# Second attention: the order of a block's direct and turned products, of VectorE's sums, and of the rows' transposes

## The chip, the cores and the metric

The kernel runs on one core of a Trainium2 chip. The metric is the device time of one execution in microseconds. A core has several engines with a queue each: TensorE (PE; its weight loads are listed as PEld), VectorE (DVE), ScalarE (ACT), GpSimd (POOL) and SyncE (SP), the last of which only starts DMAs here.

## The reference, cut to what matters

The network has a convolutional attention layer, then a plain self-attention over tokens, then a spectral filter layer. The change concerns the middle one. For each of two batches it takes normalised tokens `x` of shape 4096 x 128 and computes:

```python
scores = jnp.einsum('bsd,btd->bst', x, x)
attn_weights = jax.nn.softmax(scores, axis=-1)
return jnp.einsum('bst,btd->bsd', attn_weights, x)
```

Since queries, keys and values are the same tokens, the matrix of scores is symmetric. After the exponential, which here takes a fixed shift instead of a maximum, it still is: a 512 x 512 block (j, i) above the diagonal, turned, is the block (i, j) below it. The division by the row sums comes last.

## The kernel before, in words

The second attention is the function `attend16`. A batch has 4096 tokens in eight tiles of 512, so it has 36 blocks (j, i) with i from j to 7; 28 lie above the diagonal and 8 on it. They are numbered in the order of the list `order`: row j = 0 with i = 0 to 7, then row 1 with i = 1 to 7, and so on. The times below count the blocks of both batches through, 0 to 71.

For one block:

- `scores` works in two halves h and makes in all: twelve products `y` (three for each of four groups of 128 rows, since each operand is a sum of two half-precision parts), four exponentials `ey` on ScalarE that also give row sums into `den`, two casts to the first half-precision part of `pair` on ScalarE, and two subtractions on VectorE that give the second part (line 1199).
- `turn` (only above the diagonal) starts two transposing DMAs on SP's queue, one for each part of `pair`, into the tile `eT` (line 1204). `eT` has two buffers, `pair` two, `ey` two.
- `direct` makes twelve products `od` with `pair`, in one PSUM bank with the tag `acc1`, and adds them to `oT` for tile i on VectorE (line 1225, or a copy at 1227 in row 0).
- `across` (only above the diagonal) uses the turned block: VectorE makes four sums `both` over `eT` (line 1232), whose purpose is the row sums for `den`, and TensorE twelve products `oa` over `eT`, which add up over a row in the PSUM bank with the tag `acc0`.
- `close` ends a row j: it adds `oa` to `oT` (line 1246), sums `den` and takes reciprocals, transposes the four groups of the row on TensorE (`o`, line 1252) and adds them, scaled, to the tokens with four operations `tok` on VectorE (line 1255). It then calls `closed(j)`, which sets off or opens work for the neighbouring stages.

The loop over n runs two passes longer than there are blocks. In a pass it traces the scores and the turning of block n, then `across` of block n - 2 (and `close` where this ends a row), then `direct` of block n - 1. After each of these steps it takes one step from a generator `beside`: in batch 0 the normalising of the other batch and leftovers of the first layer, in batch 1 the feed of the third layer.

The order in which the code traces is not by itself the order in which an engine runs. The kernel is written in a framework that orders each engine's queue by rank (the order of tracing) and by the time at which it takes inputs to be there; only instructions wrapped in `keep_in_program_order` are held to the code's order on their engine. Within `attend16` none is. [...]

Of the kernel before, what the change touches and what calls it, by code (L numbers as in the profile page):

```python
# [19 lines left out]
ALU = mybir.AluOpType  # L20
# [8 lines left out]
NQ = L // 512  # L29
# [47 lines left out]
def conv_attn_hybrid(ctx: ExitStack, tc: tile.TileContext, io):  # L77
    nc = tc.nc
# [38 lines left out]
    def chain(*parts):  # L117
        for p in parts:
            yield from p
# [638 lines left out]
    def layers(st, layer0, in_halves):  # L758
# [415 lines left out]
        def attend16(b, p, beside, closed):  # L1174

            den = p.tile([P, NT, NQ], F32, tag="den", name=f"den{b}")
            oT = p.tile([P, NQ, 512], F32, tag="oT", name=f"oT{b}")

            def scores(j, i, pair, h):
                ps = psum.tile([P, 2, 512], F32, tag="st", name=f"y{b}_{j}_{i}_{h}")  # L1180
                e = p.tile([P, 2, 512], F32, tag="e", name=f"ey{b}_{j}_{i}_{h}", bufs=2)
                for q in range(2):
                    t = 4 * j + 2 * h + q
                    for n, (a, c) in enumerate(((hiT, hiT), (hiT, loT), (loT, hiT))):
                        nc.tensor.matmul(  # L1185
                            ps[:, q, :],
                            a[0][:, bass.ts(t, P)],
                            c[0][:, bass.ts(i, 512)],
                            start=(n == 0),
                            stop=(n == 2),  # L1190
                        )
                for q in range(2):
                    t = 4 * j + 2 * h + q
                    nc.scalar.activation(  # L1194
                        e[:, q, :], ps[:, q, :], AF.Exp, bias=nshift16, accum_out=den[:, t, i : i + 1]
                    )
                own = slice(2 * h, 2 * h + 2)
                nc.scalar.copy(pair[:, 0, own], e)  # L1198
                nc.vector.tensor_tensor(pair[:, 1, own], e, pair[:, 0, own], ALU.subtract)  # L1199

            def turn(j, i, pair):
                eT = p.tile([P, 2, 4, 4, P], F16, tag="eT", name=f"eT{b}_{j}_{i}", bufs=2)
                for n in range(2):
                    nc.sync.dma_start_transpose(
                        eT[:, n].rearrange("p t u k -> p (t u) k"), pair[:, n].rearrange("p t q -> p (t q)")
                    )
                return eT

            def weigh(acc, first, pair, start, stop):
                for t in range(4):  # L1210
                    own = bass.ts(first + t, P)
                    for n, (a, m) in enumerate(((hi, 0), (lo, 0), (hi, 1))):
                        nc.tensor.matmul(  # L1213
                            acc,
                            a[0][:, own],
                            pair(m, t),
                            start=(start and t == 0 and n == 0),
                            stop=(stop and t == 3 and n == 2),
                        )

            def direct(j, i, pair):
                acc = psum.tile([P, 512], F32, tag="acc1", name=f"od{b}_{j}_{i}", bufs=1)
                weigh(acc, 4 * j, lambda m, t: pair[:, m, t, :], True, True)
                if j:
                    nc.vector.tensor_tensor(oT[:, i, :], acc, oT[:, i, :], ALU.add)  # L1225
                else:
                    nc.vector.tensor_copy(oT[:, i, :], acc)

            def across(j, i, eT, acc):
                for u in range(4):  # L1230
                    both = p.tile([P, 4, P], F16, tag="both", name=f"both{b}_{j}_{i}_{u}", bufs=1)
                    nc.vector.scalar_tensor_tensor(  # L1232
                        both,
                        eT[:, 0, :, u, :],
                        1.0,
                        eT[:, 1, :, u, :],
                        ALU.mult,
                        ALU.add,
                        accum_out=den[:, 4 * i + u, j : j + 1],
                    )  # L1240
                weigh(acc, 4 * i, lambda m, u: eT[:, m, :, u, :], i == j + 1, i == NQ - 1)

            def close(j, acc):
                fin = oT[:, j, :]
                if acc is not None:
                    nc.vector.tensor_tensor(fin, acc, fin, ALU.add)
                rden = p.tile([P, 4], F32, tag="rden", name=f"rden{b}_{j}")
                nc.vector.reduce_sum(rden, den[:, 4 * j : 4 * j + 4, :], axis=AX.X)
                nc.vector.reciprocal(rden, rden)
                pt = bank(f"o{b}_{j}")  # L1250
                for t in range(4):
                    nc.tensor.transpose(pt[:, bass.ts(t, P)], fin[:, bass.ts(t, P)], ident)
                for t in range(4):
                    dst = tok[b][:, 4 * j + t, :]
                    nc.vector.scalar_tensor_tensor(
                        dst, pt[:, bass.ts(t, P)], rden[:, t : t + 1], dst, ALU.mult, ALU.add
                    )
                closed(j)

            order = [(j, i) for j in range(NQ) for i in range(j, NQ)]  # L1260
            pairs, turned, accs = {}, {}, {}
            for n in range(len(order) + 2):
                if n < len(order):
                    j, i = order[n]
                    pair = p.tile([P, 2, 4, 512], F16, tag="pair", name=f"pair{b}_{j}_{i}", bufs=2)
                    for h in range(2):
                        scores(j, i, pair, h)
                        next(beside, None)
                    pairs[n] = pair
                    if i > j:  # L1270
                        turned[n] = turn(j, i, pair)
                if n > 1:
                    j, i = order[n - 2]
                    if i > j:
                        if i == j + 1:
                            accs[j] = psum.tile([P, 512], F32, tag="acc0", name=f"oa{b}_{j}", bufs=1)
                        across(j, i, turned.pop(n - 2), accs[j])
                        if i == NQ - 1:
                            close(j, accs[j])
                    elif i == NQ - 1:  # L1280
                        close(j, None)
                    next(beside, None)
                if 0 < n <= len(order):
                    direct(*order[n - 1], pairs.pop(n - 1))
                    next(beside, None)
            for _ in beside:
                pass

# [93 lines left out]
        with ExitStack() as l1:  # L1382
# [3 lines left out]
            with ExitStack() as part:  # L1386
# [18 lines left out]
                def closed(j):  # L1405
                    gate[0] = j + 1
# [8 lines left out]
                own = (rest16(p),) if in_halves else (filters(p, fw), matrices(p))  # L1415
                steps = chain(left, stats.steps(), *own, normalise(1, stats, stage, gate))
                (attend16(0, p1, steps, closed) if in_halves else attend(0, p1, steps, closed, ready))
            right0.close()
            if in_halves:
# [274 lines left out]
        beside = chain([None] * WC, feed(1, late_pool, one_bank, fw, fed))  # L1694
        steps = 0
        for b in range(B):
            for ro in range(2):
# [3 lines left out]
                for ch in range(NCH):  # L1701
                    acc = pc.tile([P, 512], F32, tag="acc", name=f"m{b}_{ro}_{ch}")
                    for s in range(2):
                        u = f"{b}_{ro}_{ch}_{s}"
# [19 lines left out]
                beside = back(b, ro, oh, outs, late_pool)  # L1724
                if in_halves and (b, ro) == (0, 1):
                    beside = chain(beside, guard(one_bank))
# [136 lines left out]
```

## Time and profile before

| what | value |
|---|---|
| median of 3 runs | 2777.88 us (2777.81 to 2810.39) |
| the profiled execution | 2786.72 us, of which its span 2784.9 us |
| mean granted TensorE clock in it | 0.977 |
| second attention in it | about 1046 to 1724 us |
| after it | the third layer's products, which wait for a load of `tables_b` |

The page gives each engine's busy time; the answers of the trace used below give, for a stretch of the execution, the busy times by window, the waits (which instruction waited for which, in us, how often, longest), the instructions in order of time, and the chain of work that ended last. In names like `oT<-od,oT` the written tile stands to the left of the arrow. L1232 is line 1232.

### The profile page before, as it was taken

How to read it: one execution, taken by the hardware profiler on the slowest of the kernel's cores; microseconds unless marked ns; L12 is line 12 of the kernel's file. 1: busy time of each engine (PE TensorE's matmuls, PEld its weight loads, DVE VectorE, ACT ScalarE, POOL GpSimd, SP SyncE). 2: the span in 40 equal slices, each digit the busy share in tenths (PEclk: the TensorE clock that was granted, in tenths of full speed). 3: DMA queues.
4: the chain of work that ended last, by engine and by line, in shares of the span. 5: the costliest groups of instructions: out<-in, count | busy, mean ns of one | idle time of the engine just before them, and what ended most of it. 6: DMA issues, size and time to landing. Idle time of an engine off the chain costs nothing.

```text
span 2784.9 us, 32561 instructions
## 1 busy us (share of the span) xinstructions
PE 2588.1 (93%) x11955; PEld 1276.1 (46%) x11955; DVE 1668.5 (60%) x2946; ACT 1841.3 (66%) x2059; POOL 432.5 (16%) x711
## 2 busy tenths in 40 slices
PE   5999999999998996999989988898789999999998
PEld 3555555555544452444434443343344445445444
DVE  5256564246267225767886567575456666666664
ACT  4999999999998894556644555454345555555553
POOL 2022121012124201100043100111111111111110
PEclk9999999999999997999999998999999999999999
DMA  4122220012014307655375654666666666655662
GB/s 144 35 65 67 65 65 20 7 50 74 22 39 94 67 5 135 115 107 105 69 144 110 126 96 91 154 174 156 149 167 165 200 192 181 179 206 179 185 188 87
DMA packets 351051, 311.92 MB, mean 112 GB/s; under 512 B 292816, under 2 KB 303200, under 8 KB 334432
## 3 DMA queue, kind: packets, MB, share of 16 engines
q1 hardware_dynamic: 295376, 231.71, 32.6%
q0 software_dynamic: 52512, 74.81, 11.2%
q10 hardware_dynamic: 2992, 3.22, 0.4%
q8 instruction: 96, 1.57, 0.2%
q14 instruction: 75, 0.61, 0.1%
HBM read 212.53 MB, written 23.33 MB: 85 GB/s over the span
## 4 chain that ended last, share of the span: by engine, by line
PE 30%; DMA 13%; DVE 7%; issue 1%; ACT 1%; POOL 0%; SPq 0%; DVEq 0%; ACTq 0%; POOLq 0%
PE m L1557 19%; PE cv L1541 6%; DMA eT<-pair 5%; DMA tables_b<-tables 3%; DVE pair L1199 3%; DMA base<-oc 2%; DVE both L1232 2%; PE ar L1312 1%; DMA had<-base 1%; DVE x L1549 1%; PE bk L1669 1%; DMA tables_a<-tables 1%; DMA rows<-uh 1%; PE od L1213 1%; PE pf L1328 0%
## 5 line engine op out<-in xcount | busy, mean ns | idle before, releaser
L465 ACT ACTIVATE e<-s 128x1536 f16<-128x1536 f32 (+1 forms) x704 | 938.4, 1427 | 52.9 <-PE s L209 48.3
L1549 DVE TENSOR_TENSOR x<-cv,x 128x1024 f16<-128x1024 f32 x512 | 602.3, 1219 | 302.9 <-ACT x L1548 302.9
L1548 ACT CAST x<-cv 128x1024 f16<-128x1024 f32 x512 | 493.7, 1017 | 404.4 <-PE cv L1541 389.5
L1557 PE MATMUL m<-x,mxr 128*128 128x512 f16 x2048 | 622.5, 381 | 0.0
L209 PE MATMUL acc<-e,v 128*97 128x512 f16 x2048 | 559.0, 380 | 16.4 <-DVE accs L413 13.7
L209 PE MATMUL s<-qs,ks 128*128 128x512 f16 x2048 | 559.7, 380 | 7.9 <-ACT e L465 4.3
L1557 PE MATMUL m<-x,mxl 128*128 128x512 f16 x1024 | 391.4, 382 | 3.3 <-DVE oh L1564 3.2
L209 PEld LDWEIGHTS <-v 128*97 128x97 bf16 x2048 | 255.4, 125 | 229.8 <-issue 28.9
L1194 ACT ACTIVATE ey<-y,nshift 128x512 f32<-128x512 f32 x288 | 196.0, 685 | 225.3 <-PE y L1185 135.9
L1557 PEld LDWEIGHTS <-mxr 128*128 128x128 f16 x2048 | 201.3, 98 | 242.8 <-issue 5.3
L209 PEld LDWEIGHTS <-ks 128*128 128x128 f16 x2048 | 201.0, 99 | 229.6 <-issue 46.8
L1478 POOL DMA_DIRECT2D tokens<-rows x252 | 152.9, 611 | 845.5 <-PE cv L1541 819.8
L1232 DVE SCALAR_TENSOR_TENSOR both<-eT 128x512 f16<-128x512 f16 x224 | 153.6, 686 | 135.2 <-DMA eT<-pair 124.5
L1213 PE MATMUL od<-pair,hi 128*128 128x512 f16 x576 | 189.6, 391 | 30.0 <-DVE oT L1225 15.1
L1185 PE MATMUL y<-bothT 128*128 128x512 f16 x864 | 206.5, 381 | 4.0 <-ACT ey L1194 3.0
L1199 DVE TENSOR_TENSOR pair<-ey,pair 128x1024 f16<-128x1024 f32 x144 | 175.4, 1218 | 16.0 <-ACT pair L1198 15.6
L413 DVE COPY accs<-acc 97x512 f32<-97x512 f32 x64 | 44.1, 689 | 227.3 <-PE acc L209 227.1
L1541 PEld LDWEIGHTS <-tokens 128*128 128x128 f16 x1024 | 100.6, 99 | 164.5 <-issue 68.1
L1213 PEld LDWEIGHTS <-hi 128*128 128x128 f16 x1024 | 102.6, 100 | 146.2 <-issue 35.1
L1198 ACT CAST pair<-ey 128x1024 f16<-128x1024 f32 x144 | 150.2, 1043 | 24.6 <-DMA eT<-pair 11.4
L1557 PEld LDWEIGHTS <-mxl 128*128 128x128 f16 x1024 | 101.0, 99 | 131.6 <-DVE oh L1564 10.0
L1213 PE MATMUL oa<-eT,hi 128*128 128x512 f16 x448 | 146.6, 389 | 14.3 <-DMA eT<-pair 14.3
(221 smaller groups left out, 2297.5 us busy)
## 6 DMA issues: line engine op xcount, KB each, us to landing
tables_a<-tables SPq DMA_DIRECT2D x64, 1024.0 KB
tables_b<-tables SPq DMA_DIRECT2D x64, 1024.0 KB
tokens<-rows POOLq DMA_DIRECT2D x252, 128.0 KB, 12.2
tab<-in_rot SPq DMA_DIRECT2D x32, 512.0 KB
ks<-term POOLq DMA_DIRECT2D x112, 64.0 KB, 2.2
qs<-term POOLq DMA_DIRECT2D x112, 64.0 KB, 2.1
accs<-back SPq DMA_DIRECT2D x32, 128.0 KB
room<-in_mpp POOLq DMA_DIRECT2D x16, 256.0 KB, 3.4
```

The costliest lines, as they stand in the source:

```text
L209: tc.keep_in_program_order(nc.tensor.matmul(*args, **kw))
L465: nc.scalar.activation(e[:, own, :], ps[:, own, :], AF.Exp, scale=SCORE_SCALE)
L1185: nc.tensor.matmul(ps[:, q, :], a[0][:, bass.ts(t, P)], c[0][:, bass.ts(i, 512)], start=(n == 0), stop=(n == 2),)
L1194: nc.scalar.activation(e[:, q, :], ps[:, q, :], AF.Exp, bias=nshift16, accum_out=den[:, t, i : i + 1])
L1199: nc.vector.tensor_tensor(pair[:, 1, own], e, pair[:, 0, own], ALU.subtract)
L1213: nc.tensor.matmul(acc, a[0][:, own], pair(m, t), start=(start and t == 0 and n == 0), stop=(stop and t == 3 and n == 2),)
L1232: nc.vector.scalar_tensor_tensor(both, eT[:, 0, :, u, :], 1.0, eT[:, 1, :, u, :], ALU.mult, ALU.add, accum_out=den[:, 4 * i + u, j : j + 1],)
L1478: (nc.gpsimd if n else nc.sync).dma_start(ut[64 * copy : 64 * copy + 64], rows16[b].rearrange("h c r w d -> (h c) r w d")[:, row : row + B ...
L1541: ordered(nc.tensor.matmul(pu[:, h, :], ut[:, at, :], tt[:, :, at, :], start=True, stop=True))
L1548: nc.scalar.copy(hi, pur)
L1549: nc.vector.tensor_tensor(lo, pur, hi, ALU.subtract)
L1557: nc.tensor.matmul(acc, m, x, start=(s == 0 and i == 0), stop=(s == 1 and i == len(products) - 1))
```

## The change

In `across` the twelve products are traced ahead of the four sums. The final addition of a row leaves `close` and becomes a function `total`, called where `close` was. The loop traces, after the scores of block n: `close` of a row whose last block was done in the pass before, then `direct` of block n - 1, then `across` of block n - 2. The last row's `close` follows the loop. The same instructions run in both versions.

```diff
             def across(j, i, eT, acc):
+                weigh(acc, 4 * i, lambda m, u: eT[:, m, :, u, :], i == j + 1, i == NQ - 1)
                 for u in range(4):
                     both = p.tile([P, 4, P], F16, tag="both", name=f"both{b}_{j}_{i}_{u}", bufs=1)
...
-                weigh(acc, 4 * i, lambda m, u: eT[:, m, :, u, :], i == j + 1, i == NQ - 1)
-
-            def close(j, acc):
+
+            def total(j, acc):
                 fin = oT[:, j, :]
-                if acc is not None:
-                    nc.vector.tensor_tensor(fin, acc, fin, ALU.add)
+                nc.vector.tensor_tensor(fin, acc, fin, ALU.add)
+
+            def close(j):
+                fin = oT[:, j, :]
                 rden = p.tile([P, 4], F32, tag="rden", name=f"rden{b}_{j}")
...
+            whole = None
             for n in range(len(order) + 2):
...
                     if i > j:
                         turned[n] = turn(j, i, pair)
+                if whole is not None:
+                    close(whole)
+                    whole = None
+                if 0 < n <= len(order):
+                    direct(*order[n - 1], pairs.pop(n - 1))
+                    next(beside, None)
                 if n > 1:
                     j, i = order[n - 2]
                     if i > j:
...
                         across(j, i, turned.pop(n - 2), accs[j])
                         if i == NQ - 1:
-                            close(j, accs[j])
+                            total(j, accs[j])
+                            whole = j
                     elif i == NQ - 1:
-                        close(j, None)
+                        whole = j
                     next(beside, None)
-                if 0 < n <= len(order):
-                    direct(*order[n - 1], pairs.pop(n - 1))
-                    next(beside, None)
+            close(whole)
```

## The prediction

> **What bounds the kernel now.** Letters for the work of one block n (a pair j, i): S(n) its twelve score products on TensorE, P(n) its two subtractions into `pair` on VectorE, T(n) its two transposing DMAs into `eT`, D(n) its twelve direct products `od`, R(n) the add of `od` into `oT`, A(n) its twelve products `oa` over `eT`, B(n) its four sums `both`. Only blocks with i > j (28 of 36 a batch) have T, A and B. I read the busy shares first, then the waits of the stage, then the chain, then VectorE's order in the timeline.
>
> TensorE's share comes from the page. The waits are of the second attention (1045 to 1735 us): who waited, for whom, total us, times, longest.
>
> ```profile
> PE 2588.1 (93%) x11955; PEld 1276.1 (46%) x11955; DVE 1668.5 (60%) x2946; ACT 1841.3 (66%) x2059; POOL 432.5 (16%) x711
> ...
> ACT ey L1194 <- PE y L1185: 135.9, 47, 8.7
> DVE both L1232 <- DMA eT<-pair: 124.5, 43, 14.0
> ACT ey L1194 <- DVE pair L1199: 88.5, 49, 6.3
> ...
> PE od L1213 <- DVE oT L1225: 15.1, 13, 2.7
> PE oa L1213 <- DMA eT<-pair: 14.3, 5, 9.2
> ```
>
> TensorE is the busiest engine, yet the largest wait behind which work stands is VectorE's for a transposed tile. The windows (length, then TensorE busy) say what this costs TensorE:
>
> ```profile
> 1045.00:1145.00 100.00, 70.51 (x291) 30.65 (x290) 63.38 (x182) 43.41 (x90) 17.57 (x20) 0.83 0.76 130
> 1145.00:1368.00 223.00, 210.83 (x975) 96.46 (x974) 170.42 (x353) 130.74 (x270) 0.00 (x0) 0.98 0.53 100
> 1368.00:1585.00 217.00, 195.25 (x819) 90.16 (x818) 156.95 (x396) 109.86 (x226) 71.90 (x97) 0.96 0.60 121
> 1585.00:1724.00 139.00, 125.90 (x576) 56.39 (x573) 99.32 (x230) 77.77 (x161) 4.06 (x4) 0.99 0.49 92
> ```
>
> So TensorE idles 29.5, 12.2, 21.8 and 13.1 us: 76.6 us is all that any reordering could return. The second and fourth windows hold a clean loop; the chain of waits shows it (start, us, what):
>
> ```profile
> 1590.40 4.42 DMA eT<-pair
> ...
> 1594.95 0.71 DVE both L1232 x2
> ...
> 1595.68 0.70 DVE both L1232 x2
> 1596.38 1.14 DVE pair L1199
> 1597.52 0.61 DVE both L1232 x2
> 1598.13 1.14 DVE pair L1199
> ...
> 1599.29 5.94 DMA eT<-pair
> ```
>
> A transposition lands, then come two sums, P first half, a third sum, P second half, and only then can the next T go. That is 4.4 to 6 us of DMA plus 4.3 us of VectorE, 8.7 to 10.4 us a block, against TensorE's 7.77: S, A and D take 2.59 us each (S starts at 1250.84, A at 1253.43). The sums in front of P(n+1) are B(n), though the code has B(n) in the pass of n+2, after the scores of n+2. So VectorE's order isn't the code's: the framework that orders each engine's queue moved them up, taking T(n) as landed far earlier than it does. This misplaced wait is what bounds VectorE. TensorE runs ahead of it inside a row of blocks and stops at the row's end: 2.36 us before D at 1258.55, for R of the block before (one `acc1` bank).
>
> **What the Trainium skill says.** "TensorE: Matmul & The Clock Gate", section "Why this matters for your kernels", asks for no idle gap over about 3 us, or the array falls to half rate. The trace is harsher: after the 2.36 us gap the products start 0.43 us apart instead of 0.216, for about 3 us. "Perfetto Trace Analysis", section "Optimization Strategy", reads repeated bubbles as too few buffers; here both `eT` (2 buffers) and `acc1` (1) take part. "DMA: Bandwidth & Descriptors", section "DMA Transpose (X-bar)", gives this transpose to the hardware queues; all 112 stand on SP's queue, so T's second half goes behind its first, 1.96 us of issue (median).
>
> **The change, part by part.**
> *D(n-1) before A(n-2) on TensorE.* No product is added. Two things move. R comes 2.6 us sooner after its S, so the waits for R (7.1 us in the second window, 7.8 in the fourth) lose their cause. And A(n-2) ends 7.8 us after S(n) starts, instead of 5.2. `eT` has two buffers and T(n) takes the one that A(n-2) and B(n-2) release. Without stalls the last cast of block n ends 1.3 + 4 x 0.68 + 2 x 0.93 = 5.9 us after S(n) starts (half of S, four exponentials, two casts at ACT's spacing), P(n) at 7.0. Before, T(n)'s second half went at about max(7.0, 5.9 + 2.0) = 7.9. Now its first half waits for 7.8 and the second goes at about 9.8. T is 1.9 us later.
>
> *What this does to VectorE's order.* The orderer believed T(n) early enough to fit two sums, 0.73 + 0.61 = 1.3 us, before P(n+1). A shift of 1.9 us exceeds this, so B(n) should no longer be believed ready before P(n+1)'s first half. Between the halves there was room for one operation (the third sum); R(n) now is ready there and stands ahead of the sums in the code. So I expect P, R, P, then B of the block before. What the orderer charges for an issue isn't in the profile: at 2 us the shift is 1.9, at nothing 7.8 - 7.0 = 0.8 us, which leaves perhaps one sum in front. I take the first: the trace's own first block of each row, where no A lies between S and D, already has it so (R(16) at 1220.56, between the halves of P(17) at 1219.42 and 1221.16).
>
> *The loop then.* T(n) lands 9.8 + 4.4 to 6 = 14.2 to 15.8 us after S(n) starts; P(n+1) ends at 7.8 + 7.0 = 14.8, B(n) follows with at most 1 us of waiting and ends by 18.5; P(n+2) is wanted at 15.6 + 4 = 19.6. A(n) stands at 20.8. Nothing waits, and VectorE keeps TensorE's 7.77 us. VectorE's own work is 2 x 1.14 + 4 x 0.65 + 0.6 = 5.5 us a block.
>
> *B after A in the code.* They only read `eT` side by side; their rank falls below R's, as used above. Nothing else is priced.
>
> *The rows' transposes a block later.* `close` lost the final add (now `total`) and runs after the next scores. TensorE's wait for that add (4.8 us in the second window, 4.7 in the fourth, 1.1 of it before the last od products) goes. Its four `tok` operations, 4 x 0.26 = 1.0 us, leave the shadow of T and fall beside the next P: hidden while VectorE has 7.77 - 5.5 = 2.2 us to spare, 1.0 us a row if not.
>
> *Cost.* D(n) now needs P(n) 2.6 us sooner on TensorE: at 7.8 + 2.6 = 10.4 against 7.0, spare 3.4 us. Where VectorE is behind, at the first blocks of a row (T landed 5.5 to 7.2 us after P there, its halves 2 us apart), I leave 0.7 us for each of 11 row ends: 8 us; ends 0 and 20.
>
> *The other windows.* In 1045 to 1145 the DMA engines are full (share 0.76, one T issue took 17.7 us): 0, ends -3 and +3. In 1368 to 1585 the feed of the next layer stands beside; TensorE waits mostly for VectorE's `un` and `uh` (7.7 + 6.8 + 3.4 = 17.9 us), which stand in a queue whose order I can't foresee: 0, ends -12 and +12. After 1724 us a 22.2 us load of `tables_b` hangs on the last product, so the stage's end passes through whole.
>
> *Sum.* Idle time of the two loop windows 12.2 + 13.1 = 25.3, less 8, plus 2 of the 5.9 us of half-rate time (granted clock 0.98 of 223 us and 0.99 of 139 us): -19.3 us. The profiled execution took 2786.72 us (span 2784.9, so 1.8 around it) and would take 2767.4. It lies 8.8 above the median of the runs, 2777.88; off that, 2758.6.
>
> **Rivals.**
> *Same order, the wait only changes its name.* If B(n) stays ahead of P(n+1), VectorE's 8.7 us loop stays, and TensorE waits for `pair` where it waited for R. For it: TensorE's order never entered the loop. Against it: the 1.9 us. Time about 2776.
> *Slower: the same order, and TensorE's reserve is gone.* TensorE meets D(n) before P(n) is there, with a ready A(n-1) locked behind. At a row's end S of the block after next then starts 2.6 us later, less the 1.35 us that R no longer costs: 1.3 us; and the four `tok` fall into VectorE's loop: 1.0. For 11 row ends 25 us: 2803. It decides if the orderer still takes T(n) as landed before P(n+1)'s first half.
> *The feed half gains too.* If VectorE free of the wait delivers `un` and `uh` in time, 17.9 us and the 8 left come back: 2733.
>
> **How the numbers follow.** Forecast 0.55 (2745 to 2775 by its own bounds), same order 0.20, slower 0.17, feed half 0.08. The range 2730 to 2804 reaches both others. Two per cent (55.6 us, about what can be told from no change) would need almost all of the 76.6 us idle to go, or 0.8 us on each of 72 blocks: faster 0.05, within 0.87, slower 0.08.
>
> **What would show it.** Right: VectorE's wait for `eT` falls from 124.5 to under 60 us in the stage; in its timeline the sums stand behind both halves of P; the waits of `od` for R and of `o` for the add are gone; the two loop windows shrink by about 20 us together; the stage ends near 1705 us. Wrong: the sequence sum, sum, P, sum or R, P with a 3 to 5 us wait ahead of it; or a new wait of `od` for `pair`; or more half-rate products.

## The result and the profile after

Four timed executions of the changed kernel have a median of 2737.1 us (2731.29 to 2760.06), beside 2790.08 us for the kernel before in the same comparison. The ratio is 0.9842 with a 95% interval of 0.980 to 0.9883: faster by 1.6%, less than the two per cent named in the prediction. (Ratios leave out disturbed executions, so they are not quotients of the medians.) The profiled execution took 2742.39 us, its span 2740.6 against 2784.9.

TensorE's share, from the page:

```profile
PE 2579.5 (94%) x11955; PEld 1275.5 (47%) x11955; DVE 1671.6 (61%) x2946; ACT 1839.1 (67%) x2059; POOL 434.1 (16%) x711
```

The waits of the second attention (1045 to 1735 us): who waited, for whom, total us, times, longest.

```profile
ACT ey L1194 <- PE y L1185: 151.0, 62, 5.5
DVE both L1233 <- DMA eT<-pair: 46.7, 19, 11.7
...
PE od L1213 <- DVE pair L1199: 14.4, 2, 7.2
...
ACT ey L1194 <- DVE pair L1199: 13.5, 3, 6.8
...
PE oa L1213 <- DMA eT<-pair: 8.2, 3, 5.3
...
PE od L1213 <- DVE oT L1225: 2.7, 2, 1.5
```

VectorE's wait for a transposed tile fell from 124.5 to 46.7 us, and ScalarE's wait for VectorE's subtractions behind it from 88.5 to 13.5. ScalarE now waits for TensorE: the engines behind TensorE have time to spare. `od` for R fell from 15.1 to 2.7 us, and `o` for a row's final add from 9.5 to 1.4 us.

The windows at matching places (length, TensorE busy, then the other engines, granted clock, DMA share):

```profile
1045.00:1142.00 97.00, 70.92 (x300) 30.99 (x298) 67.10 (x188) 44.47 (x92) 16.34 (x20) 0.86 0.72 133
1142.00:1346.00 204.00, 203.02 (x956) 93.79 (x953) 163.82 (x332) 129.00 (x270) 0.00 (x0) 1.00 0.62 109
1346.00:1566.00 220.00, 203.04 (x875) 94.58 (x875) 171.00 (x430) 115.33 (x236) 72.72 (x98) 0.98 0.62 125
1566.00:1680.00 114.00, 113.42 (x533) 52.15 (x531) 88.95 (x207) 71.67 (x150) 5.31 (x4) 1.00 0.57 102
```

The two loop windows are full: 1.0 us idle in the second and 0.6 in the fourth, at a clock of 1.00.

That VectorE does not pass over an operation that waits is seen in the trace before. ScalarE's cast for the first half of P(19) ended at 1231.36 and VectorE was free at 1231.76, but the first sum of B(18) stood next in its queue. VectorE idled 2.13 us for the transposition, and took P(19) behind two sums:

```profile
1233.90 0.69 DVE L1232 SCALAR_TENSOR_TENSOR both<-eT 128x512 f16<-128x512 f16 x1 [2.13 <-DMA eT<-pair]
...
1235.25 1.22 DVE L1199 TENSOR_TENSOR pair<-ey,pair 128x1024 f16<-128x1024 f32 x1
```

After the change, VectorE's timeline (start, us, engine, line, operation, and in brackets the idle time ahead of it with what ended it; the small reads of an accumulator are left out) gives the order of one block:

```profile
1599.47 1.23 DVE L1199 TENSOR_TENSOR pair<-ey,pair 128x1024 f16<-128x1024 f32 x1 [0.96 <-ACT pair L1198]
1600.61 0.68 DVE L1225 TENSOR_TENSOR oT<-od,oT 128x512 f32<-128x512 f32 x1
1601.23 1.23 DVE L1199 TENSOR_TENSOR pair<-ey,pair 128x1024 f16<-128x1024 f32 x1
1603.60 0.69 DVE L1233 SCALAR_TENSOR_TENSOR both<-eT 128x512 f16<-128x512 f16 x1 [1.15 <-DMA eT<-pair]
...
1605.80 0.69 DVE L1233 SCALAR_TENSOR_TENSOR both<-eT 128x512 f16<-128x512 f16 x1
...
1607.24 1.23 DVE L1199 TENSOR_TENSOR pair<-ey,pair 128x1024 f16<-128x1024 f32 x1 [0.74 <-ACT pair L1198]
```

P, R, P, then the four sums of the block before. The wait for the transposition is 1.15 us and delays only sums; the next P waits for ScalarE, as it should. The chain of waits now runs through TensorE without a break (start, us, what), up to the load that hangs on the last product:

```profile
1610.60 2.59 PE y L1185 x12
1613.19 2.59 PE od L1213 x12
1615.78 2.59 PE oa L1213 x12
1618.37 2.59 PE y L1185 x12
...
1677.96 1.52 PE oa L1213 x7
1679.49 0.42 SPq L1491
1679.95 22.09 DMA tables_b<-tables
```

To compare kernels without fixed cuts I number the blocks of both batches 0 to 71 and take the starts of S(0), S(9), S(36), S(57), S(71) and the end of the stage's last product (a row's transpose `o`). The differences in us, with those of all the kernels below (the loops are S(9) to S(36) and S(57) to S(71)):

```
kernel                                   start   loop 1   feed    loop 2   tail   stage
before                                   99.68   223.38  225.36   116.04  14.64   679.1
after                                    94.41   207.96  216.14   102.32  13.66   634.5
after, second profile                    92.54   207.94  216.95   102.32  13.66   633.4
1  sums held behind P, nothing else      93.50   207.44  218.33   103.78  13.65   636.7
2  after, VectorE's old order by hand    98.51   237.45  236.18   120.51  17.76   710.4
3  after, three eT                       91.88   209.78  220.99   105.49  13.65   641.8
4  before, three eT                      94.23   229.87  216.78   115.80  13.97   670.7
5  D first only                          96.98   211.84  218.00   104.25  14.62   645.7
6  close later only                     101.64   211.05  218.83   106.74  13.25   651.5
7  after, all sums held behind P         94.57   206.82  211.19   102.32  13.65   628.6
8  as 7, but A ahead of D                98.92   207.20  203.29   102.32  13.25   625.0
   as 8, second profile                  95.95   207.19  203.11   102.32  13.24   621.8
```

Of the 44.6 us that the stage lost, 30.1 lie in the loops with their tail, 9.2 in the feed and 5.3 at the start. What comes after the stage took 1060.0 us before (2784.9 - 1724.90) and 1058.7 after.

### The profile page after: what moved, and what is told of

Its sections match the earlier page's. It is cut to its first block, busy times and chain, and to the rows that moved or that the text cites. A ratio compares the mean times of both kernels' runs of the same rounds, so it can differ in the third digit from the quotient of the medians.

```text
span 2740.6 us, 32562 instructions
## 1 busy us (share of the span) xinstructions
PE 2579.5 (94%) x11955; PEld 1275.5 (47%) x11955; DVE 1671.6 (61%) x2946; ACT 1839.1 (67%) x2059; POOL 434.1 (16%) x711
## 3 DMA queue, kind: packets, MB, share of 16 engines
q0 software_dynamic: 52512, 74.81, 11.7%
## 4 chain that ended last, share of the span: by engine, by line
PE 66%; DMA 14%; DVE 10%; ACT 7%; issue 2%; SPq 0%; POOL 0%; ACTq 0%; DVEq 0%; POOLq 0%
PE m L1565 18%; PE acc L209 12%; PE s L209 11%; PE cv L1549 6%; ACT e L465 5%; PE od L1213 5%; PE y L1185 4%; PE oa L1213 4%; DMA tables_b<-tables 4%; DMA tables_a<-tables 2%; DMA eT<-pair 2%; DMA had<-base 2%; DMA rows<-uh 2%; DVE pair L1199 1%; DVE x L1557 1%
## 5 line engine op out<-in xcount | busy, mean ns | idle before, releaser
L209 PEld LDWEIGHTS <-v 128*97 128x97 bf16 x2048 | 255.3, 125 | 229.9 <-issue 28.8
L1213 PE MATMUL od<-pair,hi 128*128 128x512 f16 x576 | 185.6, 383 | 19.8 <-DVE pair L1199 14.4
L1233 DVE SCALAR_TENSOR_TENSOR both<-eT 128x512 f16<-128x512 f16 x224 | 153.7, 686 | 51.6 <-DMA eT<-pair 46.7
```

What stands on the lines that cost most here:

```text
L209: tc.keep_in_program_order(nc.tensor.matmul(*args, **kw))
L1213: nc.tensor.matmul(acc, a[0][:, own], pair(m, t), start=(start and t == 0 and n == 0), stop=(stop and t == 3 and n == 2),)
L1233: nc.vector.scalar_tensor_tensor(both, eT[:, 0, :, u, :], 1.0, eT[:, 1, :, u, :], ALU.mult, ALU.add, accum_out=den[:, 4 * i + u, j : j + 1],)
```

## The experiments

Theory V: the gain is VectorE's order, B(n) no longer ahead of P(n+1), because T(n) starts later. Rival P: the gain is TensorE's order, R sooner. Rival C: the row starts set the loop, and the later `close` brings it. In the diffs `issue_after(x)` queues an operation behind x on its engine without a wait of its own, and `keep_in_program_order` queues it behind what is traced before it.

**1. VectorE's order alone.** Kernel before; a block's sums are traced a pass earlier, behind the next block's P, and held there.

```diff
+                if 0 < n <= len(order) and n - 1 in turned:
+                    sums(*order[n - 1], turned[n - 1])
...
-                    nc.vector.scalar_tensor_tensor(
+                    tc.keep_in_program_order(nc.vector.scalar_tensor_tensor(
```

> The kernel before with its own order on TensorE (A, then D) and its own close, but each block's four sums B(n) held on VectorE behind both halves of P(n+1). Theory V (the gain of the change is VectorE's order: the sums' wait for T no longer stands ahead of the subtractions that feed the next T): VectorE's wait for eT falls from 124.5 to under 60 us, the two loop windows shrink by 20 to 30 us, 2745 to 2758 us, since the waits of o for the last add of a row (about 9.5 us in all) stay. Rival P (the gain is TensorE's order: R 2.6 us sooner, so od never waits for the accumulator's bank): the waits of od for R stay, 2772 to 2785 us, whatever VectorE's wait is called.

Measured: ratio 0.9846 (0.9775 to 0.9917), stage 636.7 us, within 2.2 us of the change itself, with no product moved. The wait for `eT` in the stage:

```profile
DVE both L1232 <- DMA eT<-pair: 15.1, 13, 3.2
```

It is shorter than after the change (46.7 us) mostly in the feed, 2.7 against 23.9 us: there the framework left sums ahead of P in the changed kernel. TensorE has no wait for R in the loop windows at all, and for `o` only 1.7 us in the whole stage. V had expected about 9.5 us for `o` to stay, and with them 2745 to 2758 us; the median is 2741.89. So both waits were consequences of a late VectorE. V holds, P falls: TensorE's order isn't needed for the gain.

**2. TensorE's order with VectorE's old one.** Kernel after, with the order that VectorE had before in the steady blocks held by hand in every block.

```diff
+                    if adds:
+                        add(*adds, 0)
+                        last = add(*adds, 1)
                     for h in range(2):
-                        scores(j, i, pair, h)
+                        half = scores(j, i, pair, h, last)     # P behind `last`
+                        if adds:
+                            with after(half):                  # issue_after
+                                last = add(*adds, 2 + h)
```

> The kernel after with its order on TensorE (D, then A) and its close a block later, but VectorE's order of the kernel before held by hand: two sums of B(n), first half of P(n+1), a third sum, second half, the fourth sum. Theory V: the 8.7 to 10.4 us loop of T and VectorE is back, VectorE waits over 110 us for eT, TensorE now waits for P at D, 2776 (the prediction's rival with the same order) to 2803 us (its rival with the reserve gone). Rival P: the gain stays, 2735 to 2748 us.

Measured: ratio 1.0137 (1.0064 to 1.021), 2814.59 us in the profiled execution, stage 710.4 us. The waits of the stage:

```profile
DVE both L1235 <- DMA eT<-pair: 127.8, 48, 8.4
...
PE od L1217 <- DVE pair L1203: 33.0, 28, 7.0
PE od L1217 <- DVE oT L1229: 31.1, 11, 4.1
```

The wait for `eT` is back, and D now meets an unfinished P (33.0 us; 14.3 before) and a late R (31.1; 15.1 before). In part this is the prediction's slower rival in its place: D stands 2.6 us sooner after S, and that much of TensorE's reserve is gone. In the loops the waits for P (11.7 us) lie in the later blocks of a row and the first of the next. The waits for R there (23.3 us) are another matter. All lie at the third block of a row, 2.8 to 4.1 us each, and at the rows' starts the order held by hand is not that of before: R(16) stands behind all of P(17), and P(18) behind eight operations of `beside` and two sums, with a lag of 16.28 us against 10.17 (table under 6). V's 2776 to 2803 us is passed, with a median of 2818.58. The stage lost 31 us against before, where the rival had put 25; how much of it D ahead of A costs by itself is not separated. The change's order on TensorE without the order that it happened to cause on VectorE is no gain.

**3 and 4. A third buffer.** `bufs=2` becomes `bufs=3` for `eT`, in the kernel after and in the kernel before.

> The kernel after with three buffers for eT instead of two, so that T(n) need not wait for A(n-2). The framework then believes T(n) earlier and puts two of the four sums of B(n) ahead of P(n+1) again (they stand between the two halves). Theory V with the cause that the prediction named (the buffer's late release moved the sums): part of the gain goes, VectorE's wait for eT rises from 46.7 to 80 to 130 us, 2750 to 2780 us. Rival: a buffer more only gives T an earlier start; the loop gets slack, 2732 to 2738 us.

> The kernel before with three buffers for eT. T(n) did not wait for its buffer there (in the steady blocks it was issued 0.03 us after the last cast), and the framework's order stays two sums, P, one, P, one. Theory V: no change, the stage takes 672 to 684 us against 679, VectorE's wait for eT 110 to 135 us. Rival (the skill's reading of repeated bubbles as too few buffers): a third buffer lets T run ahead, the wait halves, under 660 us.

Measured on the kernel after: ratio 0.9863 (0.9829 to 0.9897), stage 641.8 us, 7.3 more than with two buffers, and a median of 2759.28, inside V's range; the wait in the stage, first line below, also is. On the kernel before, one execution of 2791.31 us and a stage of 670.7 us, its waits in the second fence:

```profile
DVE both L1233 <- DMA eT<-pair: 82.1, 28, 6.9
```

```profile
DVE both L1232 <- DMA eT<-pair: 116.2, 43, 6.4
...
PE od L1213 <- DVE oT L1225: 16.1, 14, 2.7
```

With three buffers after, the trace has P second half, the last two sums of B(n-1), the first two of B(n), P(n+1) first half: two of the four sums are back ahead of the P that they delay. T's first half is issued 0.02 to 0.07 us behind the last cast in every loop block. So the buffer's late release is what moved those two; that the other two stay behind with T's start set free is not explained by it, and how the framework prices them wasn't measured. In the kernel before the order stayed. Loop 1 took 6.5 us longer (229.9), loop 2 as long as before (115.8); the start was 5.5 and the feed 8.6 us shorter, which puts the stage 1.3 us below V's lower end. These differences of a single execution I can't explain. The Trainium skill, in "Perfetto Trace Analysis", section "Optimization Strategy", says that a gap which keeps repeating can mean too few buffers. Here a third buffer left the gaps in one kernel and brought some back in the other: they came from an order, not from a shortage.

**5. D(n-1) ahead of A(n-2), nothing else.**

```diff
+                if 0 < n <= len(order):
+                    direct(*order[n - 1], pairs.pop(n - 1))
+                    next(beside, None)
                 if n > 1:
```

> Of the three parts of the change only the first: D(n-1) ahead of A(n-2) in the kernel before; the sums stay in front of A in the code and a row is closed in place. The framework's order on VectorE is then the one of the kernel after in the steady blocks (half of P, four sums of the block before, half of P, R), and the row's four tok operations stand ahead of the sums. Theory V: nearly all of the gain, from y(0) of the stage to its last product 636 to 645 us (before 679, after 634.5), VectorE's wait for eT under 60 us, 2737 to 2750 us; what is left to the kernel after is only the wait of o for the last add, 4.8 and 3.6 us in the two loop windows. Rival C (the gain needs the rows' transposes a block later too, because the row starts set the loop): 655 us or more.

Measured: ratio 0.9885 (0.9802 to 0.9967), stage 645.7 us. In the steady blocks the order is P, R, P, sums, as after, and not the one in the expectation's brackets:

```profile
DVE both L1232 <- DMA eT<-pair: 58.0, 26, 12.5
...
PE od L1213 <- DVE oT L1225: 12.8, 10, 1.6
```

So this edit alone turns VectorE's order in the steady blocks, and brings three quarters of the gain (33.4 of 44.6 us; 23.4 of 30.1 in the loops with their tail). V's stage of 636 to 645 us is just missed and its time of 2737 to 2750 us clearly, with a median of 2760.29. What is left is also not what V had named: `o` waits 0.8 us for the last add, but TensorE still waits 12.8 us for R, most of it 1.6 us at a time at the third block of a row (17), where R(16) stands behind P(17), a sum and other work and VectorE lags by 10.54 us (table under 6). That wait, which the prediction had given to TensorE's order, stays with the order and goes with VectorE's lag. The remaining 11.2 us belong to the later `close` and to B behind A in the code; no run separates these two.

**6. The rows' `close` a block later, nothing else.**

```diff
+                if whole is not None:
+                    close(whole)
+                    whole = None
...
-                            close(j, accs[j])
+                            total(j, accs[j])
+                            whole = j
```

> Only the last part of the change: the kernel before with a row's close behind the next block's scores. The order of sums and subtractions stays two, P, one, P, one in the steady blocks; at a row's start one block more has P ahead of the sums. Theory V: the wait of o for the last add goes (4.8 + 3.6 us in the loop windows, and its like in the feed stretch), the wait of VectorE for eT stays over 90 us, the stage takes 660 to 675 us against 679, 2765 to 2780 us. Rival C: the row starts set the loop, 640 to 650 us.

Measured: ratio 0.9891 (0.9865 to 0.9917), stage 651.5 us: 27.6 us gained where V allowed 4 to 19, so here V's number failed and C was nearly right. (The loops with their tail gained 23.0, the feed 6.5; the start took 2.0 longer.)

```profile
DVE both L1232 <- DMA eT<-pair: 93.8, 29, 14.0
...
PE od L1213 <- DVE oT L1225: 10.2, 8, 2.3
```

The steady order is still two sums, P, sum, P, sum. How 27.6 us come back with it is seen in VectorE's lag: the end of P(n) minus the start of S(n), in us, for the third row of the first batch and the start of the fourth (the bracket is the block's row and column, counted from 0; a row's first block has no T):

```
block        before   after   1 (held)   5 (D first)   6 (close later)   2 (old order by hand)
15 (2,2)      15.30    7.56      7.56          7.56             13.97                   15.11
16 (2,3)       7.82    7.56      7.56          7.56              9.49                    9.74
17 (2,4)       9.02    7.56      8.08         10.54              7.70                   11.13
18 (2,5)      10.17    8.59      7.56          9.12              8.69                   16.28
19 (2,6)      11.40    7.58      7.56          7.56              7.56                   12.03
20 (2,7)      12.31    7.56      7.56          7.56             10.46                   12.88
21 (3,3)      14.93    7.56      7.56          7.56             13.09                   15.03
22 (3,4)      11.26    7.56      7.56          7.56             10.14                   11.24
```

Before, every block of a row adds about 1.1 us: that is the loop of T and VectorE, 8.9 us against TensorE's 7.77. TensorE doesn't feel it until the lag passes some 12 us, near the row's end (D starts 12.95 us after S when nothing holds it), and there it stops. With the close a block later the framework puts P ahead of the sums in more blocks at a row's start (17 and 19 in the table): the lag is back at 7.6 in block 19, where before it had risen to 11.4, and only blocks 20 and 21 build it up again. By the trace this edit, too, acts through VectorE's order, though no run holds that order fixed under a later `close`. A misplaced wait therefore costs what of it exceeds the reserve, and a row's start is where the account is settled.

**7 and 8. All sums held behind P.** The trace after still waits 23.9 of its 46.7 us for `eT` in the feed stretch, where the framework left sums ahead of P. Experiment 7 holds them on the kernel after; 8 does the same with A ahead of D. The lines that move D back behind A in 8 are not shown.

```diff
-                        scores(j, i, pair, h)
+                        halves[n] = scores(j, i, pair, h)      # returns P's second half
...
-                for u in range(4):
+                with tc.issue_after(half.ins):                 # half = halves[n - 1]
+                    for u in range(4):
```

> The kernel after with every block's sums B(n) held behind both halves of P(n+1), also where the framework still puts some ahead of them: in the first blocks of a batch, at the row starts and in the stretch beside the feed. Theory V: the loop windows stay as in the kernel after (they have 2 us of TensorE idle left), the stage's start and the feed stretch give some of the 26 and 17 us of TensorE idle that they still have: 2722 to 2735 us, the wait of od for pair (14.4 us at the start) under 8. Rival: those stretches wait for full DMA queues and for the feed, not for the sums; 2735 to 2742 us, or above where sums put off pile up at the rows' ends.

> The kernel after with all sums held behind both halves of P(n+1) and its close a block later, but A(n-2) ahead of D(n-1) on TensorE as before. Theory V: TensorE's order is worth nothing once the sums stand behind P; the stage takes 625 to 632 us, as with the sums held and D first (628.6). Rival P: D first has a worth of its own (R 2.6 us sooner), which the held sums had hidden: 635 us or more, with waits of od for R in the two loop windows over 5 us.

Measured: 7 has a ratio of 0.9847 (0.9778 to 0.9916), stage 628.6 us; 8 has 0.9766 (0.9692 to 0.984), stage 625.0 us. The feed from S(36) to S(57), in windows of after, 7 and 8:

```profile
1349.83:1565.97 216.14, 199.24 (x858) 92.79 (x857) 167.14 (x420) 115.33 (x236) 72.72 (x98) 0.98 0.63 128
```

```profile
1349.87:1561.06 211.19, 197.71 (x857) 93.14 (x856) 169.25 (x419) 115.24 (x236) 73.47 (x98) 0.98 0.67 131
```

```profile
1352.63:1555.91 203.28, 194.97 (x857) 92.37 (x856) 168.60 (x422) 115.07 (x236) 71.36 (x98) 1.00 0.67 136
```

TensorE idles 16.9, 13.5 and 8.3 us there. Holding the sums took VectorE's wait for `eT` in the feed from 23.9 to 1.8 us, 5.0 us off the feed and only 1.1 off the loops. That is where V looked for the gain, but V's time for 7 (2722 to 2735 us) failed: the median is 2742.27, just past the rival's 2735 to 2742. For 8, V's 625 to 632 us held and P's 635 or more did not: with the sums held, D ahead of A brings the stage nothing and costs 3.6 us. A ahead of D took another 7.9 us off the feed: TensorE's waits for `un` are 8.3 us in the feed of 7 and 2.8 in that of 8, which shows where but not why. The wait of `od` for P at the stage's start (14.4 us, two times), which V had put under 8, is the same in 7, so it isn't the sums'. That 7's total shows nothing of its 6 us is the rest of the program: 1066.8 us after the stage against 1058.7.

**9. The best version beside the kernel after**, on one chip.

> The kernel after once more, beside the version below on the same chip: ratio to the kernel before 0.980 to 0.988, the stage 630 to 640 us.

> Once more the version with A ahead of D, all sums held behind both halves of P(n+1) and the close a block later, beside the kernel after on the same chip. If what its stage showed (625.0 us against 634.5) carries to the whole, it is 5 to 13 us faster than the kernel after (ratio 0.975 to 0.981 to the kernel before); if the loads of tables after the stage swallow it, the two are within 4 us.

Measured: the kernel after 2746.22 us, ratio 0.982 (0.9768 to 0.9872); version 8 2734.14 us, ratio 0.9778 (0.9742 to 0.9815). Their stages take 633.4 and 621.8 us. The stage's 11.6 us repeat (9.5 in the first pair of profiles); the intervals of the whole overlap, so for the total I call it probable, not settled.

## Why the prediction was right and wrong

- **What bounds the kernel**: right. Taking the misplaced wait away by hand (1) gives nearly the whole gain, 42.4 of 44.6 us, and with it back (2) the gain is gone.
- **The order that follows**: right in the steady blocks, P, R, P, then B of the block before. In loop 1, from the fifth block of a row on, T(n)'s first half is issued 1.69 us behind the last cast (0.03 before), where I had 1.9; at the fourth block it is 4.3 us, at the second and third 0.03 as before. That this later start is the reason is shown for two of the four sums (3); for the other two it stays open.
- **"R comes 2.6 us sooner, so the waits for R lose their cause"**: wrong. With D first and the row closed in place (5) 12.8 us of them stay; without D first (1) they go. R was late because VectorE was.
- **The loop windows, -19.3 us**: measured -30.1. Two terms of the sum were mis-sized. The 8 us kept back for late P at row ends did not occur: `od` waits for `pair` nowhere in the loops, since the lag stays between 7.56 and 8.59 us and D starts 10.36 us after S in the steady blocks. And of the half-rate time I took back 2 us, where all came back: the clock is 1.00 in both windows. I had 5.9 us from rounded clocks; the trace before has three stretches of 3.41 us at a granted clock of 0.5 in these windows, which cost 5.1. Idle 25.3 plus 5.1 is 30.4, of which 1.6 us of idle remain. For the same reason 76.6 us of idle was not "all that any reordering could return". The Trainium skill, "TensorE: Matmul & The Clock Gate", section "Why this matters for your kernels", warns of idle gaps between bursts of products, and the trace agrees: with 1.0 and 0.6 us idle in these windows the clock is full. With the gaps gone there was no reason to keep any of the loss.
- **"The trace is harsher"**: true of some gaps only. In the trace before, a stretch at half clock follows gaps of 2.68, 2.36 and 1.22 us (that end at 1200.35, 1258.55 and 1685.16), but none follows one of 2.35 us (1610.90), nor one of 3.31 us in experiment 2 (1281.58). The length of a gap alone doesn't decide it here.
- **The later `close`**: its wait of 4.8 and 4.7 us I gave back, but not that the row starts reset VectorE's lag. Alone it is worth 27.6 us, on top of D first 11.2 with B behind A. The parts overlap: 33.4 and 27.6 make 44.6, not 61.0.
- **B behind A in the code**: priced at nothing beyond its rank; it was in no experiment by itself.
- **The feed, 0 (±12)**: -9.2, inside its bounds. `un` held TensorE 7.5 us instead of 7.7; its waits of 6.8 and 3.4 us for `uh` are gone. But the wait for `eT` in the feed still stands at 23.9 us: it is a half-mended stretch, as 7 and 8 show.
- **The start, 0 (±3)**: -5.3, but the start lies between 91.9 and 101.6 us over all kernels, without following their order; I don't count it as an effect.

So the forecast had the mechanism in the main and under half of the size: 2758.6 of 2777.88 us is a ratio of 0.9931, the measured one is 0.9842. The measured 2737.1 us lies below the forecast's own bounds (2745 to 2775), and inside the stated range only because that was drawn to take in the other cases. The time lies nearest to the fourth case, "the feed half gains too" (2733), which had been given 8 in 100. Its two parts came in part: the 8 us in full, of the feed's 17.9 us half. That the total comes so near to that case is luck: the prediction could not foresee the feed's order, and the mis-sized terms of the loops make up the rest.

## What to carry to other kernels

When a framework orders a queue, look in the timeline for a wait that stands ahead of work which doesn't need it, and hold that one operation back: this gave the gain here without moving a product. A moved step can win or lose by the order that it causes on another engine, so hold that order fixed and test the step alone. Price a lagging engine by its lag, block by block, against the reserve of the engine that sets the time, not by the sum of its waits.

## What the runs showed besides

The part of the program behind this stage is the same code in all kernels, and yet took from 1055.7 us (experiment 2) to 1076.8 us (the second profile of after) in the profiles. TensorE's waits for loads of `tables_a` and `tables_b` vary with it (21.5 us in the first profile of after, 34.2 in that of 7), but do not explain it alone: they are 32.3 us before, where this part took 1060.0. A gain of 5 to 10 us in one stage is therefore read from that stage's own marks, which repeat within 3.2 us in the two pairs of profiles here, and not from the total.
